# A mixture-of-experts loop on Trainium2: four expert loads ahead of the first gathers, and pair weights computed from visit 50 on

## The chip, the cores and the metric

The kernel runs on one core of a Trainium2 chip. A core has TensorE (matmuls, PE in the profile; its weight loads are PEld), VectorE (DVE), ScalarE (ACT), GpSimd (POOL) and SyncE (SP), and 16 DMA engines that move data between device memory and the on-chip SBUF. The metric is the device time of one execution in microseconds, less is better. Three runs of the kernel before gave 882.2, 882.6 and 886.55 us: the median is 882.6.

## The reference

The reference is a decoder of two layers on x of 8 sequences, 128 tokens and 256 features, in float32. Only its last part matters here, the mixture of experts over 1024 tokens:

```python
logits = jnp.einsum('th,eh->te', x, gate_w)          # 64 experts
probs = jax.nn.softmax(logits, axis=-1)
topk_w, topk_idx = jax.lax.top_k(probs, 8)
combine = (jax.nn.one_hot(topk_idx, 64) * topk_w[..., None]).sum(axis=1)
def step(acc, inp):
    w13_e, w2_e, c = inp
    g = x @ w13_e[:128].T
    u = x @ w13_e[128:].T
    h = jax.nn.silu(g) * u
    o = h @ w2_e.T
    return (acc + c[:, None] * o, None)
```

After it come the residual sum and a layer norm.

## The kernel before

The kernel computes only the 8192 pairs of a token and one of its eight experts. The pairs are sorted by expert into 64 blocks of 128. A *visit* takes one expert and up to 128 sorted pairs; with a block border inside an expert there are at most 127 visits, and with these inputs 104 are enough (the arm called few; the arm called all is the same with 127).

Ahead of the loop the routing stage works out which token stands in each sorted place (tok_i, L1055), which output row each place has (pairs, L1062), and the expert and start column of each visit (visits). For each pair its place is found again in slot1, and own holds the eight places of a token.

The loop, run_visits (L1103), goes over steps from -8 on. A step can do these things, and each is pipelined against the others:

- **fetch(v)** (L1123) loads an expert's three weight matrices, 384 KB, into a ring of nine tiles (wring, L1067), by a DMA from SP. It runs eight visits ahead, so the first nine fetches wait for nothing but the list of visits. A later one waits until the visit nine before it has used its tile.
- **gather(g)** (L1093) fetches the 128 token rows of block g by an indirect DMA from GpSimd. The first four are issued ahead of the loop, into tiles of their own (xg_first); the rest go into a ring of six (xg_few).
- **turn(g)** (L1117) transposes a gathered block on TensorE, and VectorE copies it to cols, the sorted columns.
- **hidden(v)** (L1136) does gate and up on TensorE (8 matmul records), silu on ScalarE, and the product hid (moe_h_few, L1152) on VectorE.
- **down(v)** (L1155), two steps later, does the last matmuls (4 records) and ScalarE copies the result back to cols (L1162).
- **turn_back(g)** (L1166), from step 43 on, transposes a finished block on TensorE, VectorE copies it to moe_os, and an indirect DMA from GpSimd scatters its rows to pair_rows in device memory.
- **weight(b)** and **spread(b)** (L1070, L1085), at every twelfth step, compute for sequence b on VectorE the weights of its pairs: eq (two 128x512 operations, L1072 and L1076), a reduction to pair_weight (L1079), and five 128x128 diagonal matrices, diag (L1087).

TensorE's and GpSimd's orders in the loop are as written (manual_schedule, L1182). VectorE's is not: a scheduler places its instructions by when their inputs are ready. The inputs of weight(b) are ready before the loop, so all eight groups stand among the first twenty or so visits there, with two eq ahead of the first copy to cols. In TensorE's order turn(0) and turn(1) stand ahead of hidden(0); behind it come turn(2), hidden(1), turn(3), hidden(2), turn(4) and down(0).

Behind the loop the tail reads pair_rows back (z), sums the eight rows of each token with the weights, and finishes. It uses diag and pair_weight.

Of the kernel before, what the change touches and what calls it, by code (L numbers as in the profile page):

```python
# [14 lines left out]
ALU = mybir.AluOpType  # L15
# [3 lines left out]
B = 8  # L19
# [15 lines left out]
NG = B * S * TOP // P  # L35
NV = NG + NE - 1
AHEAD = 4
FEW = 104
FAR = 65536.0
MIDDLE = (P - 1) / 2  # L40
# [19 lines left out]
def decoder_kernel(ctx: ExitStack, tc: tile.TileContext, i, out):  # L60
    nc = tc.nc
# [23 lines left out]
    def ps_mm(name):  # L85
        return ps_of["mm"].tile([P, 512], F32, tag="mm", name=name)

    def ps_tr(name):
        return ps_of["tr"].tile([P, 512], F32, tag="tr", name=name)

    def ps_o(name):
        return ps_of["o"].tile([P, 512], F32, tag="o", name=name)
# [389 lines left out]
    with l0, tc.tile_pool(name="l0a", bufs=2) as ap:  # L482
# [4 lines left out]
        qT, kT, v = [], [], []  # L487
# [582 lines left out]
    def weight(b):  # L1070
        eq = wk.tile([P, TOP, NE], F32, tag="e", bufs=6, name=f"eq_{b}")
        nc.vector.tensor_tensor(  # L1072
            eq, slot1[:, b, :].unsqueeze(1).to_broadcast([P, TOP, NE]),
            own[:, b, :].unsqueeze(2).to_broadcast([P, TOP, NE]), ALU.is_equal,
        )
        nc.vector.tensor_tensor(  # L1076
            eq, eq, comb[:, b, :].unsqueeze(1).to_broadcast([P, TOP, NE]), ALU.mult
        )
        nc.vector.reduce_sum(cw[:, b, :], eq, axis=AX.X)  # L1079
# [5 lines left out]
    def spread(b):  # L1085
        for k in range(ON_PE):
            nc.vector.tensor_scalar(diag[:, b, k, :], ident, cw[:, b, k : k + 1], None, ALU.mult)  # L1087

    def turned(step):

        return min(max(step + 3 + max(step, 0) // 4, 0), NG)

    def gather(g, arm, x=None):  # L1093
        if x is None:
            x = mp.tile([P, D], F32, tag="xg", bufs=6, name=f"xg_{arm}_{g}")
        nc.gpsimd.indirect_dma_start(  # L1096
            out=x, out_offset=None, in_=xd,
            in_offset=bass.IndirectOffsetOnAxis(ap=tok_i[:, g : g + 1], axis=0),
            bounds_check=B * S - 1, oob_is_err=False,
        )  # L1100
        return x

    def run_visits(arm, count):  # L1103


        spare = count - NG

        def begins(v, engine, after):

            with tc.issue_after(after[-1]) if after else nullcontext():  # L1110
                return nc.values_load(
                    visits[0:1, 1, v : v + 1], engines=[engine],
                    min_val=max(v - spare, 0) * P, max_val=min(v, NG) * P,
                    skip_runtime_bounds_check_because="each visit before takes 128 pairs at the most",
                )

        def turn(g):  # L1117
            pt = ps_tr(f"moe_xT_{arm}_{g}").rearrange("p (k t) -> p k t", k=4)[:, :2]
            for k in range(2):
                nc.tensor.transpose(pt[:, k, :], xg[g][:, k * P : (k + 1) * P], ident)  # L1120
            nc.vector.tensor_copy(cols[:, :, (g + 1) * P : (g + 2) * P], pt)  # L1121

        def fetch(v):  # L1123
            w = wring.tile([P, 3 * D], F32, tag="w", name=f"w_{arm}_{v}")
            with tc.issue_after(fetched[-1]) if fetched else nullcontext():
                e = nc.values_load(
                    visits[0:1, 0, v : v + 1], engines=[nc.sync.engine], min_val=0, max_val=NE - 1,
                    skip_runtime_bounds_check_because="the least of it and the last expert was taken",
                )
                dma = nc.sync.dma_start(  # L1130
                    out=w, in_=i["experts"][:, bass.ds(e, 1), :].rearrange("p e n -> p (e n)")
                )
            fetched.append(dma.ins)
            ws[v] = w

        def hidden(v):  # L1136
            o = begins(v, nc.tensor.engine, fed)
            ps = ps_mm(f"moe_gu_{arm}_{v}")[:, :D].rearrange("p (a t) -> p a t", a=2)
            for a in range(2):
                for k in range(2):  # L1140
                    at = k * D + a * P
                    mm = nc.tensor.matmul(  # L1142
                        ps[:, a, :], ws[v][:, at : at + P], cols[:, k, bass.ds(o + P, P)],
                        start=(k == 0), stop=(k == 1),
                    )

                    tc.declare_no_dep(mm.ins, group=f"left_{arm}", reason="columns of earlier visits")
            fed.append(mm.ins)
            s = mp.tile([P, P], F32, tag="s", name=f"moe_s_{arm}_{v}")
            nc.scalar.activation(s, ps[:, 0, :], AF.Silu)  # L1150
            hid = mp.tile([P, P], F32, tag="hid", bufs=4, name=f"moe_h_{arm}_{v}")
            nc.vector.tensor_tensor(hid, ps[:, 1, :], s, ALU.mult)  # L1152
            hs[v] = hid

        def down(v):  # L1155
            ps = ps_o(f"moe_o_{arm}_{v}")[:, :D].rearrange("p (c t) -> p c t", c=2)
            for c in range(2):
                at = 2 * D + c * P
                nc.tensor.matmul(ps[:, c, :], ws[v][:, at : at + P], hs[v], start=True, stop=True)  # L1159
            o = begins(v, nc.scalar.engine, left)  # L1160

            cp = nc.scalar.copy(cols[:, :, bass.ds(o, P)], ps)  # L1162
            left.append(cp.ins)
            tc.add_to_no_dep_group(f"left_{arm}", cp.ins)

        def turn_back(g):  # L1166
            pt = ps_tr(f"moe_oT_{arm}_{g}")[:, :D]
            for k in range(2):
                nc.tensor.transpose(pt[:, k * P : (k + 1) * P], cols[:, k, g * P : (g + 1) * P], ident)  # L1169
            o = mp.tile([P, D], F32, tag="o", bufs=4, name=f"moe_os_{arm}_{g}")  # L1170
            nc.vector.tensor_copy(o, pt)  # L1171
            inst = nc.gpsimd.indirect_dma_start(  # L1172
                out=zd, out_offset=bass.IndirectOffsetOnAxis(ap=pairs[:, g : g + 1], axis=0),
                in_=o, in_offset=None, bounds_check=B * TOP * S - 1, oob_is_err=False,
            )

            tc.declare_no_dep(inst.ins, group=f"pairs_{arm}", reason="disjoint rows")
            tc.add_to_no_dep_group(f"pairs_{arm}", inst.ins)

        fed, left, fetched = [], [], []  # L1180
        xg, ws, hs = dict(ahead), {}, {}
        with tc.manual_schedule(engines={nc.tensor.engine, nc.gpsimd.engine}):  # L1182
            for step in range(-8, count + 4):
                if 0 <= step < count:
                    hidden(step)
                for g in range(turned(step - 1), turned(step)):
                    turn(g)
                if 0 <= step - 2 < count:
                    down(step - 2)
                if 0 <= step + 8 < count:  # L1190
                    fetch(step + 8)
                while len(xg) < min(turned(step) + 4, NG):
                    xg[len(xg)] = gather(len(xg), arm)
                if 0 <= step - 3 - spare < NG:
                    turn_back(step - 3 - spare)
                if 0 <= step < 12 * B and step % 12 == 11:
                    weight(step // 12)
                    spread(step // 12)

    ahead = {  # L1200
        g: gather(g, "first", wk.tile([P, D], F32, tag=("r", "xb")[g % 2], name=f"xg_first_{g}"))
        for g in range(AHEAD)
    }
    few = nc.values_load(
        visits[0:1, 2, FEW : FEW + 1], min_val=0, max_val=NE,
        skip_runtime_bounds_check_because="a number of experts",
    )
    with tc.If(few == NE) as enough:
        run_visits("few", FEW)
    with enough.Else():  # L1210
        run_visits("all", NV)
# [11 lines left out]
    for b in range(B):  # L1223
        z = zs[b]
        ps = ps_mm(f"moe_sum_{b}")[:, :D]
# [81 lines left out]
```

## Time and profile before

| what | value |
|---|---|
| median of three runs | 882.6 us |
| profiled execution, its own time | 881.06 us |
| its span, first to last instruction | 879.1 us |
| granted TensorE clock, mean | 0.954 |
| TensorE busy | 803.5 us, 91% |
| VectorE busy | 460.3 us, 52% |
| GpSimd busy | 232.9 us, 26% |
| expert loads | 104 of 384 KB |
| first expert load issued | 620.16 us |
| first matmul of visit 0 | 634.51 us |
| last scatter issued | 840.23 us |

Times in the profile count from the start of the span. A row of the timeline has the start, the length, the engine, the line, the operation, the tile written and those read; in brackets stands how long the engine was idle before it and what ended that. A DMA row on SP or GpSimd is the issue of a transfer, not the transfer itself. In a table by stretch the first figures are busy microseconds of each engine with the number of instructions.

### The profile page before, as it was taken

What the parts mean: (1) busy time and instruction counts of PE and PEld (TensorE: products, weight loads), DVE (VectorE), ACT (ScalarE), POOL (GpSimd) and SP (SyncE); (2) the same over time, 40 slices, a digit from 0 to 9 for tenths busy, and PEclk for the clock granted to TensorE, in tenths of its full rate; (3) what the DMA queues carried; (4) which work ended last, traced back from release to release, by engine and by line L of the source; (5) the groups of instructions that cost most, each with busy time, mean ns of one, the idle gap of its engine ahead of it and who ended that gap; (6) DMA issues with size and microseconds to landing.
All of it is one profiled execution on the core that took longest, in us unless ns stands there. A gap on an engine that the chain in (4) does not pass through costs nothing. (4 is left out here: it accounts for less than half of the span.)

```text
span 879.1 us, 14286 instructions
## 1 busy us (share of the span) xinstructions
PE 803.5 (91%) x4588; PEld 539.6 (61%) x4588; DVE 460.3 (52%) x1280; ACT 288.7 (33%) x990; POOL 232.9 (26%) x321
## 2 busy tenths in 40 slices
PE   8899997999999999999999999996588888999945
PEld 5455653667455558555557655553588877988834
DVE  3699886413544442344444566755795333443335
ACT  2567742221333330233330132332232332333301
POOL 0011113215100000000015121101566655555524
PEclk9999987999999999999999998987599999999979
DMA  5500011820000000000000000000579987998665
GB/s 167 157 1 1 2 48 49 293 90 1 0 1 0 1 1 0 1 0 1 1 18 31 1 14 1 13 13 13 198 227 287 296 279 224 299 309 290 203 237 228
DMA packets 39730, 87.80 MB, mean 100 GB/s; under 512 B 6432, under 2 KB 16192, under 8 KB 38752
## 3 DMA queue, kind: packets, MB, share of 16 engines
q1 hardware_dynamic: 32352, 68.96, 24.0%
q0 software_dynamic: 6144, 16.79, 5.7%
q10 hardware_dynamic: 1152, 1.05, 0.4%
q8 instruction: 41, 0.67, 0.3%
q14 instruction: 41, 0.34, 0.1%
HBM read 76.29 MB, written 10.49 MB: 99 GB/s over the span
## 5 line engine op out<-in xcount | busy, mean ns | idle before, releaser
L224 ACT ACTIVATE l_e<-l_s,nm_l 128x128 f32<-128x128 f32 x256 | 90.4, 370 | 93.2 <-DVE nm_l L221 92.9
L1142 PE MATMUL moe_gu_few<-cols,w_few 128*128 (+1 forms) x832 | 114.0, 281 | 2.2 <-issue 0.4
L1142 PEld LDWEIGHTS moe_gu_few<-cols,w_few 128*128 128x128 f32 x832 | 102.9, 195 | 7.5 <-issue 6.6
L1172 POOL DMA_INDIRECT pair_rows<-moe_os_few,pairs x64 | 63.3, 988 | 53.3 <-DVE moe_os_few L1171 41.1
L1096 POOL DMA_INDIRECT xg_few<-x_rows,tok_i x60 | 62.8, 1047 | 29.5 <-issue 11.3
L1159 PE MATMUL moe_o_few<-moe_h_few,w_few 128*128 128x128 f32 x416 | 63.9, 276 | 0.0
L843 ACT ACTIVATE y_e<-y_sT 128x512 f32<-128x512 f32 x64 | 33.0, 603 | 83.3 <-PE y_sT L836 50.6
L740 PE MATMUL l_q<-xT_l1a,w_qkv 128*128 128x512 f32 x128 | 60.2, 593 | 0.0
L740 PE MATMUL l_k<-xT_l1a,w_qkv 128*128 128x512 f32 x128 | 60.1, 592 | 0.0
L740 PE MATMUL l_v<-xT_l1a,w_qkv 128*128 128x512 f32 x128 | 60.1, 592 | 0.0
L231 DVE TENSOR_SCALAR l_e<-l_e,inv_l 128x128 f32<-128x128 f32 x256 | 58.3, 292 | 1.4
L723 DVE TENSOR_TENSOR l_vs<-l_c,l_vs 128x512 f32<-128x512 f32 x32 | 22.1, 692 | 67.4 <-PE l_c L722 67.4
L1162 ACT COPY cols<-moe_o_few 128x256 f32 (+1 forms) x104 | 38.9, 374 | 55.2 <-PE moe_gu_few L1142 18.7
L703 PE MATMUL l_y<-w_o,l_vs 128*128 128x256 f32 x256 | 56.9, 381 | 0.0
L1150 ACT ACTIVATE moe_s_few<-moe_gu_few 128x128 f32<-128x128 f32 x104 | 28.9, 279 | 79.9 <-PE moe_gu_few L1142 39.8
L1159 PEld LDWEIGHTS moe_o_few<-moe_h_few,w_few 128*128 128x128 f32 x416 | 55.2, 193 | 0.0
L703 PEld LDWEIGHTS l_y<-w_o,l_vs 128*128 128x128 f32 x256 | 48.2, 190 | 9.8 <-issue 2.8
L224 ACT ACTIVATION_READ_ACCUMULATOR l_e<-l_s,nm_l 128x1 f32 x256 | 53.2, 208 | 0.0
L1121 DVE COPY cols<-moe_xT_few 128x256 f32<-128x256 f32 x64 | 26.5, 417 | 48.2 <-PE moe_o_few L1159 21.4
L1152 DVE TENSOR_TENSOR moe_h_few<-moe_gu_few,moe_s_few 128x128 f32<-128x128 f32 x104 | 29.7, 286 | 41.5 <-ACT moe_s_few L1150 25.6
L221 DVE TENSOR_REDUCE nm_l<-l_s 128x4 f32<-128x512 f32 x64 | 43.2, 684 | 10.0 <-PE l_s L755 8.1
L748 ACT COPY l_vs<-l_v 128x512 f32<-128x512 f32 x32 | 18.8, 586 | 78.4 <-PE l_v L740 78.4
(267 smaller groups left out, 1360.0 us busy)
## 6 DMA issues: line engine op xcount, KB each, us to landing
w_few<-in_experts SPq DMA_DIRECT2D x104, 384.0 KB
z<-pair_rows SPq DMA_DIRECT2D x7, 1024.0 KB
w_qkv<-in_w_qkv SPq DMA_DIRECT2D x8, 768.0 KB
w_o<-in_w_o SPq DMA_DIRECT2D x1, 2048.0 KB
xT<-in_xT SPq DMA_DIRECT2D x2, 512.0 KB
x<-in_x SPq DMA_DIRECT2D x4, 256.0 KB
cx<-in_ctx SPq DMA_DIRECT2D x1, 1024.0 KB
q_up<-in_up_qT SPq DMA_DIRECT2D x4, 256.0 KB
```

The lines of the kernel that those rows point to most:

```text
L221: nc.vector.tensor_reduce(nm, s, AX.X, ALU.max, negate=True)
L224: nc.scalar.activation(e[:, a, :], s[:, a, :], AF.Exp, bias=nm[:, a : a + 1], scale=1.0, accum_out=sums[:, a : a + 1],)
L231: nc.vector.tensor_scalar(e[:, a, :], e[:, a, :], inv[:, a : a + 1], None, ALU.mult)
L703: nc.tensor.matmul(py[:, :D], scaled[b // 4, m][:, b % 4 * S : (b % 4 + 1) * S], w_o[:, m, :], start=(m == 0), stop=(m == L1_HEADS - 1),)
L740: nc.tensor.matmul(ps, w_qkv[:, k, c, n, :], xT[h][:, k, :], start=(k == 0), stop=(k == 1))
L843: nc.scalar.activation(e, tiles[j], AF.Exp)
L1096: nc.gpsimd.indirect_dma_start(out=x, out_offset=None, in_=xd, in_offset=bass.IndirectOffsetOnAxis(ap=tok_i[:, g : g + 1], axis=0), bounds ...
L1142: mm = nc.tensor.matmul(ps[:, a, :], ws[v][:, at : at + P], cols[:, k, bass.ds(o + P, P)], start=(k == 0), stop=(k == 1),)
L1152: nc.vector.tensor_tensor(hid, ps[:, 1, :], s, ALU.mult)
L1159: nc.tensor.matmul(ps[:, c, :], ws[v][:, at : at + P], hs[v], start=True, stop=True)
L1162: cp = nc.scalar.copy(cols[:, :, bass.ds(o, P)], ps)
L1172: inst = nc.gpsimd.indirect_dma_start(out=zd, out_offset=bass.IndirectOffsetOnAxis(ap=pairs[:, g : g + 1], axis=0), in_=o, in_offset=None, ...
```

## The change

It has three parts, and the rest of the kernel is as before.

First, fetch(4) is preceded by a memset of one element of its tile on GpSimd. In GpSimd's order this stands behind the four gathers of xg_first and ahead of the first one of xg_few. The load overwrites the element, so it has to wait for the memset; the fetches behind it on SP follow it.

Second, weight and spread of sequence b move from step 12b + 11 to step 50 + 6b, that is to steps 50, 56, up to 92.

Third, each such group is placed behind the product hid of the latest visit in VectorE's order (issue_after of the last entry of gated). Otherwise the scheduler orders VectorE as before.

```diff
+PROMPT = 4
...
         def fetch(v):
             w = wring.tile([P, 3 * D], F32, tag="w", name=f"w_{arm}_{v}")
+            if v == PROMPT:
+
+                nc.gpsimd.memset(w[0:1, 0:1], 0.0)
             with tc.issue_after(fetched[-1]) if fetched else nullcontext():
...
-            nc.vector.tensor_tensor(hid, ps[:, 1, :], s, ALU.mult)
+            gated.append(nc.vector.tensor_tensor(hid, ps[:, 1, :], s, ALU.mult).ins)
...
-        fed, left, fetched = [], [], []
+        fed, left, fetched, gated = [], [], [], []
...
-                if 0 <= step < 12 * B and step % 12 == 11:
-                    weight(step // 12)
-                    spread(step // 12)
+                if 0 <= step - 50 < 6 * B and (step - 50) % 6 == 0:
+
+                    with tc.issue_after(gated[-1]):
+                        weight((step - 50) // 6)
+                        spread((step - 50) // 6)
```

In VectorE's order of the changed kernel the first instruction of the loop is a copy to cols; each group then stands as hid, eq, a copy to moe_os, eq times combine, the reduction, the next hid, and five diag.

## The prediction

> **What bounds the kernel now.** I read the page's chain of waits first, then a table of busy time in stretches, then the timeline of the stretch where the expert loop starts. The chain puts the loop's matmuls first, but it begins with a transfer of experts, a gather, and VectorE:
>
> ```profile
> 622.93 3.65 DMA w_few<-in_experts
> 626.62 0.62 POOL xg_first L1096
> ...
> 628.24 5.75 DMA xg_first<-x_rows,tok_i
> ...
> 634.03 0.70 PE moe_xT_few L1120 x2
> 635.18 1.20 DVE eq L1076 x2
> ...
> 638.38 0.98 DVE diag L1087 x5
> ```
>
> Columns: start, length, what. A gather issued at 628.24 has landed only at 633.99, and from there VectorE's work on the pair weights (eq, diag) is on the chain. The table by stretch (window, length, then busy us of PE, PEld, DVE, ACT, POOL, then the granted clock, DMA share, GB/s):
>
> ```profile
> 620.00:630.00 10.00, 5.36 (x44) 5.03 (x42) 7.70 (x16) 2.90 (x4) 3.17 (x4) 0.50 0.82 282
> 630.00:640.00 10.00, 6.29 (x37) 5.60 (x38) 5.85 (x18) 1.76 (x4) 7.87 (x8) 0.65 0.52 182
> 640.00:650.00 10.00, 9.52 (x81) 8.98 (x81) 9.21 (x30) 3.11 (x10) 6.41 (x7) 1.00 0.71 207
> 650.00:660.00 10.00, 7.73 (x64) 6.88 (x62) 10.00 (x31) 3.06 (x10) 7.27 (x7) 1.00 0.84 277
> 660.00:690.00 30.00, 27.25 (x232) 25.87 (x232) 15.03 (x50) 9.35 (x31) 19.97 (x20) 1.00 0.91 292
> ```
>
> VectorE is full from 640 to 660 and half idle afterwards. The timeline of GpSimd's and VectorE's rows there:
>
> ```profile
> 626.62 1.32 POOL L1096 DMA_INDIRECT xg_first<-x_rows,tok_i  x1 [6.22 <-DMA w_few<-in_experts]
> 628.24 1.00 POOL L1096 DMA_INDIRECT xg_first<-x_rows,tok_i  x1 [0.30 <-issue]
> 629.55 1.52 POOL L1096 DMA_INDIRECT xg_first<-x_rows,tok_i  x1 [0.30 <-issue]
> 631.37 1.00 POOL L1096 DMA_INDIRECT xg_first<-x_rows,tok_i  x1 [0.30 <-issue]
> 632.67 1.00 POOL L1096 DMA_INDIRECT xg_few<-x_rows,tok_i  x1 [0.30 <-issue]
> ...
> 651.09 1.70 POOL L1096 DMA_INDIRECT xg_few<-x_rows,tok_i  x1 [0.83 <-PE moe_gu_few L1142]
> ```
>
> The reader is to see that gathers go out back to back, one per 1.30 us (1.00 and a gap of 0.30), and that some take longer.
>
> Two things that the averages hide. **Expert weights are not what TensorE waits for**: in the trace's packets, from visit 9 on, each expert's 384 KB land 5.7 us or more before its visit. And **VectorE is hardly what sets the pace**: starts of visits in the trace are 2.01 us apart from visit 4 to 18 (669.95 - 641.87, over 14), where VectorE is full, and still 1.94 from 18 to 42 (716.59 - 669.95, over 24), where it isn't. What remains there is the ring of six gather buffers: a gather lands about 3.7 us after its issue, TensorE turns it two or three us later, and GpSimd waits 0.8 to 1.0 us for that every two or three gathers. After visit 50 visits are 1.74 us apart.
>
> **Part 1: loads 4 to 8 behind the first gathers.** Before, the nine loads that fill the ring are issued between 620.16 and 627.41, so gather 0 (issued 626.62) is in the DMA queues with loads 5 to 8 and lands at 631.98, 5.4 us after its issue. Gather 5, issued at 633.98 when the loads were done, took 2.4 us. After, load 4 waits for a memset that stands in GpSimd's queue behind the four gathers. Nothing else stands on SP behind load 4 but loads 5, 6 and so on. Loads 0 to 3 land by 626.18 as before, so gather 0 meets empty queues and lands at about 629.0, gather 1 (628.24) at 630.7, gather 2 at 632.0, gather 3 (issued 630.9, since gather 2 loses its excess of 0.5) at 633.3.
>
> The memset: a 1x1 one is not in the trace; the nearest row is GpSimd's 128x256 memset of cols, 0.31 us, so it costs between 0 and 0.6 us with its gap. With it gather 4 goes out near 632.3, where it went at 632.67. Load 4 starts near 632.2 and lands, with the 3.6 us that load 4 takes now, near 636; its visit is at 641.87 now, at about 639 after. The cover shrinks from 14 us to 3. Load 8 follows at 635.9 and lands by 642 for a visit near 646.
>
> Down the path: transposes 0 and 1 go from 633.16 and 634.03 to about 629.2 and 630.8, visit 0 from 634.36 to about 631.3. Then the table load on ScalarE (1.28 us) and the first two hid follow. Ahead of visit 0's second matmuls in TensorE's order stands the transpose of gather 4, now at 639.32. That gather now travels among loads 4 and 5: 2.4 us if they leave it alone, 5.4 at worst, so it lands between 634.7 and 637.7; I take 636.2, by the middle of both rows. Gain there: 3.0 us (1.5 to 4.0).
>
> Here a rule speaks against the change. The Trainium skill, "DMA: Bandwidth & Descriptors", section "SWDGE vs HWDGE vs iDMA", says that inside each DMA engine the software and the hardware queues are different ones and taken in turn. By it a gather passes the backlog of loads, and part 1 would win little, at most the doubled transfer time, 0.7 us. The row says otherwise: gather 0's first packet starts 3.9 us after its issue, gather 5's 1.7. I go by the row: 3.0 and not 0.7.
>
> **Part 2: pair weights away from visits 0 to 20.** Removed there are 8 groups of eq (0.68), eq times combine (0.67), reduce (0.67) and 5 diag (0.28): spaced as they are (0.60 and 0.20), 2.8 us each, 22 us of VectorE. By the pace of visits this is worth (2.01 - 1.94) x 14 = 0.9 us; the bounds are 0 and 2.3 us, the sum by which gathers 10 to 22 exceed 1.00. I take 0.9. What is late next is the ring of gathers, which doesn't change.
>
> **Part 3: the same groups behind visits 50, 56, ... 92.** The copies of gathers into cols end at 739.5, so VectorE is 15.7 us busy in the 65 us from 741 to 806 (TensorE's copies back and hid), and a group adds 2.8 us to each 10.4. In the changed order eq stands behind hid(50), then one copy to moe_os, eq times combine and reduce, hid(51), 5 diag. hid(51) is late by up to 1.2 us and one copy by 0.7. In the trace a regular visit has 2.0 us between the start of hid and the matmul that needs it (hid of visit 74 at 781.75, its matmul at 784.35), and a scatter has 1.25 us of idle GpSimd behind every second one. So most is hidden; without that cover a group costs up to 1.2, eight 9.6.
>
> What is not hidden is GpSimd. Here I weigh the second rule: "SBUF — State Buffer", section "Who interferes with whom", lets tensor_tensor and tensor_reduce leave descriptor generation alone, and makes fp32 tensor_scalar block it. By that the diag instructions would cost: 5 x 0.2 x 8 = 8 us. The rows say that the gather at 651.09 took 1.70 beside an eq (651.24), while the one at 654.83 took 1.00 beside four diag (654.63 to 655.49), and every gather between 663 and 718 took 1.00. The excess over 1.00 of all gathers from the third on is 3.2 us. I take half of it as on the path, since GpSimd is idle in part: **+1.6** (0 to 3.2; 9.6 if VectorE's delays count too).
>
> **Sum**: -3.0 - 0.9 + 1.6 = -2.3 us. The profiled execution took 881.06 (span 879.1), so it would take 878.8; the median shown is 1.5 above it, 882.6, hence **880.3**.
>
> **Rivals.**
> 1. *Both gains are whole and VectorE's late work free*: -4.0 - 2.3 + 0 = -6.3, 876.3. For it: DMA share is 0.52 and 0.71 in the stretches that would fill, and all slack above. Against it: with a full VectorE the pace was only 3% worse.
> 2. *The start doesn't carry*: what gather 0 wins, gathers 4 to 9 lose among the five late loads (5 x 1.3 us of transfer from 632 to 639), and the ring of gathers sets the pace anyway: 0 to -0.5, 882.4.
> 3. *Slower*: from visit 50 VectorE's groups stand between hid and TensorE. TensorE's waits there come in lumps (visit 77 starts 3.0 us after 76, visit 84 3.1 after 83), with ScalarE, VectorE and GpSimd all released together; behind such a lump the cover of 2 us is gone and the whole delay counts. At 1.2 us a group, 9.6 - 3.9 = +5.7: 888.3. It decides from (3.9 + 4.4) / 8 = 1.04 us a group on.
> That the change is undone by a scheduler is no case: in the changed program the groups do stand behind hid 50, 56 and so on, and load 4 has its wait for GpSimd.
>
> **How the numbers follow.** The forecast 0.42, rival 1 0.24, rival 2 0.17, rival 3 0.17. Half a per cent, 4.4 us, is about what a measurement here can tell. Faster is below 878.2: nearly all of rival 1 and a fifth of the forecast, 0.32. Slower is above 887.0: most of rival 3, 0.16. Within: 0.52. The forecast's own range is 877 to 883 (its unknowns: 1.5 to 4.0, 0 to 2.3, 0 to 3.2). To leave out no more than 2 in 10 the range reaches through rival 1 and most of rival 3: 874.5 to 888.5.
>
> **What would show it.** Right: the first gather landed before 630, transposes 0 and 1 before 631, visit 0 before 632, transpose 4 near 636; load 9 near 638 rather than 641.45; gathers between 641 and 661 all at 1.00; visits 4 to 18 at 1.95 us; scatters of 1.2 to 1.7 beside eq after visit 50, and visits 50 to 92 at most 0.05 us slower each. Wrong: transpose 4 after 638.5 (part 1), visit 42 less than 3 us earlier than now (part 2), or the time from visit 50 to 103 (94.4 us now) longer by more than 4 us (part 3).

## The result, and the profile after

The changed kernel took **886.45 us** (median of 20 runs) beside 882.0 us for the kernel before (20 runs): a ratio of 1.0058, 95% interval 1.0040 to 1.0077. It is slower by 0.6%, where the prediction said 880.3 and no change. The profiled execution took 887.66 us.

The same stretches as before (length, then busy us of PE, PEld, DVE, ACT, POOL, then the granted clock, DMA share, GB/s):

```profile
620.00:630.00 10.00, 5.49 (x43) 4.92 (x40) 6.20 (x13) 2.90 (x4) 3.19 (x4) 0.50 0.55 183
630.00:640.00 10.00, 6.38 (x38) 5.52 (x38) 2.28 (x6) 1.84 (x3) 7.22 (x9) 0.84 0.79 253
640.00:650.00 10.00, 10.00 (x77) 10.00 (x77) 3.75 (x12) 3.26 (x11) 5.67 (x6) 0.83 0.80 243
650.00:660.00 10.00, 9.22 (x79) 8.60 (x78) 3.13 (x11) 2.84 (x10) 6.28 (x7) 1.00 0.91 298
660.00:690.00 30.00, 26.20 (x221) 24.65 (x221) 11.24 (x36) 9.52 (x32) 18.94 (x19) 1.00 0.90 285
```

VectorE (third figure), which was full from 640 to 660, is now busy for a third. Yet TensorE does 77 and 79 matmul records there, where it did 81 and 64, and from 660 to 690 it does 221, where it did 232. From 640 to 690 that is 377 records in both: the room on VectorE turned into nothing.

The start of the loop, from the timeline of all engines:

```profile
630.66 0.69 PE L1121 MATMUL moe_xT_few<-ident,xg_first 128*128 128x128 f32 x2 [0.52 <-DMA xg_first<-x_rows,tok_i]
631.14 1.92 PE L1146 MATMUL moe_gu_few<-cols,w_few 128*128 128x128 f32 x8
631.45 0.09 POOL L1128 MEMSET w_few<- 1x1 f32 x1
...
633.19 1.06 PE L1146 MATMUL moe_gu_few<-cols,w_few 128*128 x8
...
634.55 0.41 PE L1121 MATMUL moe_xT_few<-ident,xg_first 128*128 128x128 f32 x2 [0.30 <-issue]
...
635.29 1.13 PE L1146 MATMUL moe_gu_few<-cols,w_few 128*128 x8 [0.32 <-DVE moe_h_few L1156]
...
637.80 0.28 ACT L1154 ACTIVATE moe_s_few<-moe_gu_few 128x128 f32<-128x128 f32 x1 [3.01 <-PE moe_o_few L1163]
...
639.27 0.42 DVE L1122 COPY cols<-moe_xT_few 128x256 f32<-128x256 f32 x1 [0.87 <-remote]
...
639.75 1.95 PE L1146 MATMUL moe_gu_few<-cols,w_few 128*128 x8 [2.44 <-issue]
640.80 0.28 ACT L1154 ACTIVATE moe_s_few<-moe_gu_few 128x128 f32<-128x128 f32 x1 [2.73 <-PE moe_gu_few L1146]
```

Visit 0 starts 3 us earlier than before, as forecast. Then look at visit 1: its eight records start at 633.19 and end at 634.25 by the profile's model, and ScalarE, idle from 634.79, starts the silu on them only at 637.80, 3.5 us after that end. For visit 2 (635.29 to 636.42) it is 640.80, 4.4 us. VectorE is late in the same way: it copies transpose 3, which ended at 634.96, to cols only at 639.27 (the trace can't name who ended that wait). Visit 3 needs this copy, so it waits until 639.75, and the lead is gone. Its eight records then take 1.95 us in place of 1.06: the granted clock was 0.51 from 640.0 to 643.4, where it was 1.00 before.

The late stretch, as one row each: before first, then after (740 to 833, between visits 50 and 103 in both).

```profile
740.00:833.00 93.00, 87.89 (x732) 82.15 (x731) 36.78 (x105) 32.38 (x104) 51.26 (x52) 1.00 0.85 278
```

```profile
740.00:833.00 93.00, 83.88 (x690) 77.44 (x689) 53.77 (x162) 31.01 (x98) 49.38 (x49) 1.00 0.88 273
```

VectorE has 17 us more to do, and TensorE gets 690 records done in place of 732. The visits behind one late group (it began at 751.41 with eq behind hid, and ended at 755.75 with the last diag), from the timeline:

```profile
758.50 1.06 PE L1146 MATMUL moe_gu_few<-cols,w_few 128*128 x8
...
760.95 0.61 PE L1163 MATMUL moe_o_few<-moe_h_few,w_few 128*128 128x128 f32 x4
762.18 0.28 ACT L1154 ACTIVATE moe_s_few<-moe_gu_few 128x128 f32<-128x128 f32 x1 [3.21 <-PE moe_o_few L1163]
...
762.76 0.37 ACT L1166 COPY cols<-moe_o_few 128x256 f32 x1 [0.31 <-ACT moe_s_few L1154]
...
763.19 0.44 PE L1173 MATMUL moe_oT_few<-ident,cols 128*128 128x128 f32 x2 [1.63 <-ACT cols L1166]
```

Again silu begins 2.6 us after the modelled end of its matmuls (759.56), the copy to cols comes behind it, and TensorE, whose transpose of a finished block needs that copy, stands for 1.63 us. Where all this went is plain when the starts of visits are counted from the first expert load (us):

| | visit 0 | 4 | 18 | 42 | 50 | 103 | visits 50 to 103 |
|---|---|---|---|---|---|---|---|
| before | 14.21 | 21.71 | 49.79 | 96.44 | 119.24 | 213.64 | 94.40 |
| after | 11.15 | 22.79 | 49.46 | 97.07 | 119.33 | 219.52 | 100.19 |

Up to visit 50 nothing is won, and then 5.8 us are lost.

### The profile page after: what moved, and what is told of

It is laid out like the page before. It is cut to its first block, busy times and chain, and to the rows that moved or that the text cites. A ratio compares the mean times of both kernels' runs of the same rounds, so it can differ in the third digit from the quotient of the medians.

```text
span 885.7 us, 14292 instructions
## 1 busy us (share of the span) xinstructions
PE 804.0 (91%) x4588; PEld 539.1 (61%) x4588; DVE 458.3 (52%) x1280; ACT 288.6 (33%) x990; POOL 230.4 (26%) x322
## 5 line engine op out<-in xcount | busy, mean ns | idle before, releaser
L1176 POOL DMA_INDIRECT pair_rows<-moe_os_few,pairs x64 | 64.3, 1005 | 58.3 <-DVE moe_os_few L1175 28.4
L1097 POOL DMA_INDIRECT xg_few<-x_rows,tok_i x60 | 59.9, 999 | 33.5 <-PE moe_gu_few L1146 15.3
L1166 ACT COPY cols<-moe_o_few 128x256 f32 (+1 forms) x104 | 38.8, 373 | 50.6 <-PE moe_o_few L1163 16.6
```

The costliest lines, as they stand in the source:

```text
L1097: nc.gpsimd.indirect_dma_start(out=x, out_offset=None, in_=xd, in_offset=bass.IndirectOffsetOnAxis(ap=tok_i[:, g : g + 1], axis=0), bounds ...
L1176: inst = nc.gpsimd.indirect_dma_start(out=zd, out_offset=bass.IndirectOffsetOnAxis(ap=pairs[:, g : g + 1], axis=0), in_=o, in_offset=None, ...
```

## The experiments

The ratio is always against the kernel before, run beside it on the same chip, with its 95% interval. The experiments ran on five chips. The kernel before took 880.9, 878.4 and 877.7 us on those of the first, second and fourth, but 853.9 and 853.5 on those of the third and fifth. That turned out to be the key, so stages are compared within one kind of chip only. "Late" below means: silu begins more than 0.8 us after the modelled end of its gate and up matmuls.

### First chip: the parts alone

**The start alone** (groups at every twelfth step as before, memset kept).

> The kernel before with the memset alone (loads 4 to 8 behind the first gathers); the pair weights stand where they stood. Bunching theory (GpSimd's indirect DMAs, standing back to back while other DMA traffic runs, hold back TensorE's completions): visit 0 starts about 3 us earlier than before, the lead is lost again by visit 5 to a wait at visits 3 and 4, visits 50 to 103 take 94 to 95 us as before, total -1.5 to +1 us. If the lead had been lost to the late groups alone, the total would be 3 us below before. If the memset is what made the kernel slower, it is 4 to 6 us above before.

Measured: 0.9998 (0.9980 to 1.0015). Visit 0 stands at 11.18 us and visit 4 at 22.44: the lead is lost between them. Visits 50 to 103 took 96.10 us, a little over the 94 to 95 expected. Part 1 is worth nothing.

**The late groups alone** (the changed kernel without its memset).

> The changed kernel without the memset: all nine loads in front again, pair weights from visit 50. Bunching theory: visits 50 to 103 take 99 to 101 us as in the changed kernel (94.4 before), visits 4 to 42 save about 1 us, total 4 to 5.5 us above before. If memset and late groups share the loss, the total is 1 to 3 us above before.

Measured: 1.0055 (1.0030 to 1.0080), visits 50 to 103 100.38 us. The whole loss is here.

**No groups.** The groups are left out, and diag and pair_weight set to zero behind the loop, so the experts' sum is missing from the output.

> The changed kernel with the eight groups of pair weights left out; diag and pair_weight are set to zero behind the loop, in time that VectorE waits for pair_rows, so the experts' sum is left out of the output. Both the bunching theory and the direct theory (VectorE's groups make TensorE wait for hid): visits 50 to 103 back to 93 to 95 us, total 5 to 7 us below the changed kernel, about 0 to 1.5 us below before. If the longer end is due to the shifted start (memset) and not to the groups, visits 50 to 103 stay at 98 to 101 us.

```diff
     loop.close()
+    nc.vector.memset(diag, 0.0)
+    nc.vector.memset(cw, 0.0)
```

Measured: 1.0040 (1.0022 to 1.0059). The scheduler put the 128x5120 memset (4.33 us) at 605.3, ahead of the routing's work on VectorE, so the total says nothing. Visits 50 to 103 took 95.32.

**Groups in lumps, but early** (behind hid at steps 6, 11, to 41).

> The changed kernel with the groups at steps 6, 11, ... 41 instead of 50, 56, ... 92, each still behind the latest hid. Bunching theory: visits 50 to 103 take 94 to 95 us; in visits 6 to 42 the gathers wait for TensorE and not for VectorE, so a group costs at most 0.3 us there: total -1 to +2 us against before. Direct theory: a group costs its 0.7 us there too, the total stays 4 to 6 us above before.

Measured: 1.0051 (1.0035 to 1.0066). Visit 50 is at 123.17 (119.33 in the changed kernel), and visits 50 to 103 take 95.45. Against the start alone, which has the same memset, the early lumps cost 3.5 us (885.68 - 882.21); against the kernel before, the late ones cost 4.5 (885.43 - 880.92). So a lump costs at both places, as the direct theory had it and the bunching theory had not.

### Second chip: what of a late group costs

**No groups, cleanly**: loads as before, the two memsets behind the last copy to moe_os.

> Loads at the start as in before, the groups of pair weights left out altogether (diag and pair_weight are set to zero by two memsets behind the last copy to moe_os, beside the last scatter), so the output is not the reference's. It gives the price of the late groups by difference, with nothing moved ahead of the loop. Theory (the late groups cost about 5 us): visits 50 to 103 take 94 to 96 us, as in before and 4 to 6 less than in the changed kernel; visits 4 to 18 take 1.90 us each; all in all 0.998 of before (880 to 881). Rival (the 5 us come from something else in the late stage, such as where the loads stand in the ring): visits 50 to 103 take 99 us or more here too, and the ratio is 1.003 or more.

Measured: 1.0005 (0.9984 to 1.0026), visits 50 to 103 94.77, visits 4 to 18 1.85 us each (2.005 in before), but visit 4 at 23.38 (21.71). The ratio expected was 0.998. So on this chip, where the groups stood before, they cost nothing that shows in the time, and there was nothing to win by moving them.

**The same, with scatters four at a time**:

> The same without groups, but GpSimd's scatters are put out four at a time: each fourth turned block sends its own scatter and those of the three before it; moe_os has eight buffers. VectorE does nothing more than in the run without groups. Theory H (a row of scatters without pause holds back what TensorE reports to ScalarE and VectorE; the late groups cost what they cost because they bunch the scatters): visits 50 to 103 take 98 us or more, with waits of TensorE of 1 to 2 us at each row of four, and the ratio is 1.003 or more. Theory D (the groups stand in front of hid and of the copies to moe_os on VectorE, and that alone is what TensorE waits for): visits 50 to 103 stay within 1 us of the run without groups, 94 to 96.

```diff
+            held.append((g, o))
+            if len(held) < HELD and g < NG - 1:
+                return
+            for g, o in held:
...
```

Measured: 0.9974 (0.9962 to 0.9987), visits 50 to 103 93.96. Theory H, that the scatters need only stand in rows to do harm, falls: here they helped a little.

**Groups taken apart**, one part behind each hid from visit 50 to 89:

> The groups are taken apart: behind the hid of each visit from 50 to 89 stands one part only (eq; eq times combine; the reduction; three diag; two diag), five visits for a sequence. The same work on VectorE in the same stretch, at most 0.84 us between two hid in place of 1.2 to 2.8. Loads as in before. If the cost is that of lumps (delay beyond TensorE's cover, or bunched scatters): visits 50 to 103 take 94.5 to 97 us and the ratio is 1.000 or less. If it is the sum of VectorE's time, or GpSimd's longer scatters beside eq: 98.5 us or more and 1.003 or more.

```diff
-                if 0 <= step - 50 < 6 * B and (step - 50) % 6 == 0:
+                if 50 <= step < 50 + 5 * B:
                     with tc.issue_after(gated[-1]):
-                        weight((step - 50) // 6)
-                        spread((step - 50) // 6)
+                        part((step - 50) // 5, (step - 50) % 5)
```

Measured: 0.9996 (0.9979 to 1.0014), visits 50 to 103 94.99. The same work in the same stretch costs nothing when it isn't in a lump. That excludes the sum of VectorE's time, and the longer scatters beside eq, as the cost.

**Loads from the fourth on behind gather 7** (groups as before):

> Groups at every twelfth step as in before; the memset that lets load 4 go stands behind gather 7 in place of gather 3, so gathers 4 to 7 go out with no load of an expert in flight. If the stall at visits 3 and 4 (4.5 and 2.8 us in the changed kernel) comes from gathers going out back to back while loads are in flight: visit 3 starts at most 2.5 us after visit 2, transpose 4 goes within 2.5 us of its gather's landing time of about 635, and visit 4 stands at 20 to 21.5 us from the first load (22.4 with the memset behind gather 3, 21.7 in before), unless load 4 itself is late, which shows as a wait for w_few. If the stall is that of the gathers alone or of ScalarE's table load: visits 3 and 4 stay where they were, 22.4 or later. Ratio by the first 0.998, by the second 1.000 to 1.002.

Measured: 1.0006 (0.9991 to 1.0021). The memset is at 635.96 and load 4 goes out at 636.13. Silu of visit 1 is on time and visit 3 starts 1.6 us after visit 2, as the first theory has it; but silu of visit 2, due at 635.14, begins at 638.28, and visit 4 starts 4.8 us after visit 3, at 21.86. The stall moved back by one visit and did not go. It was already there for a microsecond when the load went out, so whether loads have a part in it is left open; in the time nothing is won.

### Third chip: the same lumps where ends are not late

**The kernel before with scatters in fours**, **whole late lumps with scatters in fours** (loads as before), **the weights in a lump with one diag a visit**, and **the weights one a visit with the diag in a lump**:

> The kernel before, with its groups at every twelfth step and its loads as they are, and only GpSimd's scatters put out four at a time with eight buffers for moe_os. The run without groups gained 0.3% by that. If the gain belongs to the scatters alone: ratio 0.9975 (0.996 to 0.999), visits 42 to 50 take 20.5 us (22.8 in before) and 50 to 103 at most 94. If it needed VectorE's free time at the start: 1.000.

> The late groups in lumps as in the changed kernel, loads as in before, and scatters four at a time with eight buffers for moe_os. Theory G (a lump costs because the copies to moe_os are held back, the scatters then stand in a row and hold each other and what waits for GpSimd): with scatters in rows anyway and eight buffers the lumps cost at most 1 us, visits 50 to 103 take 94 to 95.5, ratio 0.9975. Theory D (hid or the copies come too late for TensorE, whatever GpSimd does): visits 50 to 103 take 98.5 us or more, ratio 1.003.

```diff
                 if 0 <= step - 50 < 6 * B and (step - 50) % 6 == 0:
                     with tc.issue_after(gated[-1]):
                         weight((step - 50) // 6)
                         spread((step - 50) // 6)
...
+            held.append((g, o))
+            if len(held) < HELD and g < NG - 1:
+                return
```

> Loads as in before. In place of a whole group behind hid 50, 56 and so on, the eq, eq times combine and the reduction stay together (2.04 us between two hid, with one copy to moe_os among them), and the five diag follow one a visit. If the three operations of the weights are what costs (hid late by 1.2 us): visits 50 to 103 take 98.5 to 100 us and the ratio is 1.004 or more. If it needs the whole lump, or the diag: 94.5 to 96.5, ratio 1.000.

```diff
+                if 50 <= step < 50 + 6 * B:
+                    b, n = divmod(step - 50, 6)
+                    with tc.issue_after(gated[-1]):
+                        if n == 0:
+                            weight(b)
+                        else:
+                            spread(b, n - 1)
```

> The counterpart: eq, eq times combine and the reduction stand one a visit, and the five diag together (1.06 us, one copy to moe_os among them). If the diag cost (GpSimd held by fp32 tensor_scalar, or the copy behind them): visits 50 to 103 take 98 us or more. If the weights do: 94.5 to 96 and ratio 1.000.

```diff
+                if 50 <= step < 50 + 6 * B:
+                    b, n = divmod(step - 50, 6)
+                    with tc.issue_after(gated[-1]):
+                        part(b, n)
```

Measured: 0.9974 (0.9961 to 0.9987), **0.9931** (0.9907 to 0.9955), 0.9942 (0.9917 to 0.9967) and 0.9950 (0.9930 to 0.9970). The last three are lower than any theory had said. Visits 50 to 103 take 83.16, 83.11, 83.80 and 83.70 us, against 94 to 100 so far, and the lump costs nothing. The timeline of the whole late lump with fours, at its first group:

```profile
720.75 0.68 DVE L1074 TENSOR_TENSOR eq<-slot,own 128x512 f32<-128x512 f32 x1
721.35 0.42 DVE L1173 COPY moe_os_few<-moe_oT_few 128x256 f32<-128x256 f32 x1
...
722.25 1.06 PE L1144 MATMUL moe_gu_few<-cols,w_few 128*128 x8
...
723.00 0.28 DVE L1154 TENSOR_TENSOR moe_h_few<-moe_gu_few,moe_s_few 128x128 f32<-128x128 f32 x1
...
723.35 0.28 ACT L1152 ACTIVATE moe_s_few<-moe_gu_few 128x128 f32<-128x128 f32 x1 [0.61 <-PE moe_gu_few L1144]
...
723.81 1.06 PE L1144 MATMUL moe_gu_few<-cols,w_few 128*128 x8
...
724.71 0.50 PE L1161 MATMUL moe_o_few<-moe_h_few,w_few 128*128 128x128 f32 x3
```

Silu begins at 723.35, 0.04 us after the modelled end of its matmuls (723.31). Hid is late by the group, at 723.00 with silu done at 722.07, but the matmul that needs it is due only at 724.71: the cover that the prediction counted on is there. TensorE starts a visit every 1.56 us and does not wait. The same in one row for 81 us:

```profile
720.00:801.00 81.00, 81.00 (x725) 80.66 (x725) 56.20 (x168) 33.85 (x104) 52.68 (x52) 1.00 0.92 320
```

725 records in 81 us without a pause, at the same granted clock of 1.00 as the 690 in 93 us of the changed kernel. In the four profiles of this chip silu is late at visit 0 alone (the table load); from visit 50 on its mean delay is 0.04 us. In the profile of the kernel before at the head of this document it is late at 23 of the 24 visits from 18 to 41 and at 7 of the 54 from 50 on; in the changed kernel at 24 and 15.

The other finding is on the start: with the groups at the start (scatters in fours) visits 4 to 18 take 1.91 us each and visit 50 stands at 103.30; with late groups 1.71 and 99.30. On this chip the groups' early place did cost 4 us.

### Fourth chip: the lumps where ends come late

> The changed kernel once more, beside the next three. Theory L (a lump costs only where TensorE's ends are reported late): where silu begins 0.1 us or less after its matmuls, visits 50 to 103 take 83 to 84.5 us, as in the last runs, and the ratio is 0.992 to 0.996; where it begins 1 us or more after them at ten or more of the visits from 50 on, they take 99 to 100.5 and the ratio is 1.005. Rival (the lump of a whole group always costs, the last runs were free because their lumps were smaller or their scatters came in fours): 4 us more than the run with the spread groups of this batch, whatever silu does.

> Whole lumps, scatters four at a time with eight buffers, on the chip of this batch. Theory L: as the changed kernel, so 98.5 us or more for visits 50 to 103 where silu begins late, 83 to 84.5 where it doesn't. Theory G (scatters held one behind the other by late copies to moe_os make the cost): at least 3 us less than the changed kernel for visits 50 to 103 where silu begins late there.

> The weights in a lump, diag one a visit, on the chip of this batch. Where silu begins late, the size of the lump decides: 97 to 100 us for visits 50 to 103 and 1.003 or more if 2 us of VectorE are enough, 94.5 to 96 and 1.000 if only the whole lump costs. Where silu doesn't begin late: 83 to 84.5 and 0.994, as in the run before.

**Spread groups and scatters in fours**:

> One part of a group behind each hid from visit 50 to 89, and scatters four at a time: both edits that cost nothing or gained alone. If their effects add: 0.9975 where silu begins late (the gain of the scatters), 0.993 or less where it doesn't (that of VectorE's free time at the start too).

| kernel | median, us | ratio (95%) | visits 50 to 103 | late from visit 50 on |
|---|---|---|---|---|
| changed kernel | 883.49 | 1.0063 (1.0043 to 1.0084) | 99.43 | 18 |
| whole lumps, fours | 881.62 | 1.0032 (1.0013 to 1.0052) | 100.63 | 18 |
| weights in a lump | 878.41 | 1.0011 (0.9994 to 1.0027) | 95.73 | 8 |
| spread, fours | 876.59 | 0.9990 (0.9975 to 1.0005) | 94.46 | 4 |

Theory L holds, and theory G falls: the very kernel whose lumps were free on the third chip loses 6.2 us here against the one with spread groups (100.63 - 94.46), 5.0 by the medians, 0.63 us a group. Both have their scatters in fours and no memset. (The changed kernel's own time on this chip would not have told theory L from its rival.) Most of the loss shows at one group of instructions, the transposes of finished blocks. Columns: busy us, mean ns, then TensorE's idle time ahead of them and who ended it; whole lumps with fours on this chip (736 to 834), then the spread groups with fours (736 to 827), then the whole lumps on the third chip (720 to 801):

```profile
L1171 PE MATMUL moe_oT_few<-ident,cols 128*128 128x128 f32 x104 | 20.7, 280 | 8.2 <-ACT cols L1164 7.8 <-issue 0.4
```

```profile
L1172 PE MATMUL moe_oT_few<-ident,cols 128*128 128x128 f32 x102 | 20.3, 281 | 1.6 <-ACT cols L1165 1.0 <-issue 0.5
```

```profile
L1171 PE MATMUL moe_oT_few<-ident,cols 128*128 128x128 f32 x104 | 19.9, 273 | 0.0
```

7.8, 1.0 and 0.0 us of waiting for ScalarE's copies to cols: 6.8 us between the first two kernels, about what the visits lost. (Where TensorE waits is not always the same place: the spread groups with single scatters, on the second chip, also waited 6.6 us there, and less ahead of the gate and up matmuls. The time of the visits is the firm figure.) A lump of the weights alone (2.04 us of VectorE, single scatters) stands 1.3 us above the spread groups by the visits, and by the time nothing that can be told: the cost of 5 us needs the whole group. The effects of the spread groups and of the fours did not surely add: 0.9975 was expected, 0.9990 measured.

### Fifth chip: what makes the ends late

> The kernel before, with each finished block written by a plain DMA from SP to consecutive rows in place of GpSimd's scatter (the rows stay unsorted, so the output is not the reference's). No indirect DMA is left from visit 56 or so on; the bytes are the same. If GpSimd's indirect DMAs make TensorE's ends late, and the chip is one where they are: silu begins 0.1 us after its matmuls from visit 56 on and visits 50 to 103 take 83 to 86 us (94.4 in before). If they don't: as before, 93 to 96, with silu 1 us or more late at five visits or more. On a chip without late ends: 83 to 84 in any case.

```diff
-            inst = nc.gpsimd.indirect_dma_start(
-                out=zd, out_offset=bass.IndirectOffsetOnAxis(ap=pairs[:, g : g + 1], axis=0),
...
+            inst = nc.sync.dma_start(out=zd[g * P : (g + 1) * P, :], in_=o)
```

> The kernel before, but from visit 50 on no expert is loaded: the visits use the nine tiles of visits 41 to 49 in turn (the output is not the reference's). GpSimd's scatters stay. If loads in flight make TensorE's ends late, or make the scatters' descriptors slow, and the chip is one where they are late: silu begins 0.1 us after its matmuls from visit 52 on and visits 50 to 103 take 83 to 86 us. If the scatters alone do it: 93 to 96. If both are needed, this run and the one with SP's writes both fall to 83 to 86. If neither matters, both stay at 93 to 96, and what is left is TensorE itself.

```diff
         def fetch(v):
+            if v >= 50:
+                ws[v] = ws[41 + (v - 41) % 9]
+                return
```

Measured: 0.9977 (0.9963 to 0.9992) and 0.9986 (0.9972 to 1.0001). This chip was of the second kind: silu was never late but at visit 0, visits 50 to 103 took 82.63 and 82.59. So neither run could tell what makes ends late; what the traces show of it stands in the last section. The two do show that on such a chip neither GpSimd's scatters nor the expert loads hold the late stage: with both, on the third chip, it took 83.2 us, and TensorE hardly paused.

## Why the prediction was wrong

**Part 1's first steps were right, its gain was not.** The first gather landed at 628.99 (forecast 629.0), transposes 0 and 1 went at 629.45 and 630.66, visit 0 at 630.93, and transpose 4 at 636.42 (forecast 636); only load 9, at 640.90, was 3 us later than said. With no loads ahead of it gather 0's first packet came 2.0 us after its issue (3.9 before), so the reading of the row held, and not what was made of the rule weighed there. The step that failed is "Gain there: 3.0 us (1.5 to 4.0)": what a gain at visit 0 is worth at the end was taken for the gain itself. By visit 3 it was gone, because ScalarE and VectorE took up TensorE's results 3.5 to 4.4 us late. The start alone measured 0.9998. Rival 2 had the outcome, not the mechanism: gathers 5 and 6 had landed at 637.13 and 638.12, and were turned at 641.28 and 643.83, so it was not they that TensorE waited for.

The clock is a term that the sum does not have. Five of the six profiles with the memset show a stretch of 3.4 or 6.8 us at a granted clock of 0.5 that begins 8.8 to 12.3 us after visit 0; none of the fourteen without it does. It is not what loses the lead: the sixth, the first of the runs without groups, shows no such stretch and has visit 4 at 23.19.

**Part 2's 0.9 us came and went.** The gathers from 641 to 661 all took 1.00, and visits 4 to 18 took 1.905 each, as expected or better. But visit 42 came 0.6 us later in place of 3 earlier (from the first load), and without any groups the time is 1.0005. The step that failed is the reading that the ring of gather buffers sets the 1.94 us of visits 18 to 42: on the third chip the same ring allows 1.61 to 1.67. What stood in that stretch was silu, 1 to 2.5 us late at nearly every visit. It takes VectorE's place as soon as VectorE is free: in visits 9 to 17 silu was late once before, and eight times after. Where it isn't late, the prediction erred the other way: VectorE did set the pace, and 4 us were to be had, not 0.9 or 2.3.

**Part 3 was mis-sized: +1.6 was forecast, about +5 was measured** (5.8 between the two profiles, 5.0 by the medians on the fourth chip). The step that failed is "What is not hidden is GpSimd". A scatter took 1005 ns in the mean after and 988 before, about 1 us over all 64, and the spread groups have the same scatters (1007 ns) at no cost. Hid itself stayed covered, as the prediction said. TensorE's groups from 740 to 833, two of before and then the same two of after, with its idle time ahead of them last:

```profile
L1159 PE MATMUL moe_o_few<-moe_h_few,w_few 128*128 128x128 f32 x208 | 31.7, 275 | 0.0
L1169 PE MATMUL moe_oT_few<-ident,cols 128*128 128x128 f32 x104 | 20.7, 280 | 3.7 <-ACT cols L1162 3.2 <-issue 0.5
```

```profile
L1163 PE MATMUL moe_o_few<-moe_h_few,w_few 128*128 128x128 f32 x197 | 30.1, 275 | 0.0
L1173 PE MATMUL moe_oT_few<-ident,cols 128*128 128x128 f32 x98 | 19.3, 279 | 7.2 <-ACT cols L1166 6.2 <-issue 1.1
```

Ahead of the matmuls that read hid (moe_o) TensorE never waited. What grew is its wait for ScalarE's copies to cols ahead of the transposes, a path through late silu that the prediction put at nothing. Counted from the starts of all records between visits 50 and 103 (0.112 us apart where nothing is waited for), the waits ahead of the transposes grew from 5.1 to 9.6 us, those at gate and up from 5.6 to 7.0, which together is about the loss.

Two readings in that part are off, too. The 15.7 us of VectorE from 741 to 806 are the copies to moe_os alone; with hid they are 26.4. The two times given for visit 74 are 2.6 us apart, not 2.0. The rule of the Trainium skill, "SBUF — State Buffer", section "Who interferes with whom", by which fp32 tensor_scalar such as diag can block descriptors, is not borne out either: in the spread kernel 14 scatters stand beside diag alone and took 0.98 each, while those beside eq alone took up to 1.40.

Rival 3 had the outcome and the kind of place, waits in lumps in which ScalarE, VectorE and GpSimd are all released together. Its mechanism, "the cover of 2 us is gone and the whole delay counts", is not what the trace shows: the first hid behind a lump has 1.7 us from its start to its matmul, in the changed kernel (visit 51) as on the third chip, where the lumps cost nothing. That its 888.3 lies close is in part luck: 1.2 us a group was too much (0.63 measured), and the gains of 3.9 set against it did not exist.

That a lump and late ends together make the loss is shown, by one kernel on two kinds of chip and by the spread groups. How a lump brings about more late ends (15 from visit 50 on, 7 before) is not: the spread groups with single scatters also had 15, and lost nothing. How much of a late end is passed on to TensorE must differ, and no run here took that apart.

**A version that beats both?** Scatters four at a time gained 0.26% twice, once without groups and once on a chip without late ends. With spread groups, on a chip with late ends, they came to 0.999 (0.9975 to 1.0005), 0.8% under the changed kernel (876.59 and 883.49) but not surely under the kernel before. On a chip without late ends whole late groups with fours gained 0.7%. The changed kernel itself was not run on such a chip.

## What to carry to other kernels

Work that is moved into an engine's idle time is better put there in small parts: here the same eight groups cost 5 us in lumps of 2.8 us and nothing one part a visit (at most 0.84 us). That the direct consumer of a delayed result has cover does not mean that the other paths have: hid was never waited for, the copy to cols was. Look first at how long after its matmuls the engine that reads TensorE's result begins, because a loop in which that is late gives back what is gained at its head. And a change worth half a per cent may change its sign with the chip (the whole late lumps with fours: 1.0032 and 0.9931), so compare stages on one chip only.

## What was not expected of the hardware

On three chips, and on that of the first profiles too by its trace, ScalarE and VectorE take up TensorE's results 1 to 6 us after the modelled end of the matmuls, at most visits from 18 to 42 and at some later. On two others they do it within 0.04 us, and the kernel before takes 853.5 to 853.9 us in place of 877.7 to 882.0. The granted clock is the same (mean 0.954 in the first profile of before and in that of before with fours on the third chip), the first expert load goes out at nearly the same time (620.16 and 617.97), and the tail behind the last scatter takes 38.8 and 38.4 us: nearly the whole difference lies in the expert loop.

The ends of matmuls are modelled, but the trace has the times at which TensorE's reports arrive, the updates of the semaphore that the other engines wait for. Behind the late group shown above none arrives from 759.91 to 762.15, then five within 0.25 us, for matmuls that had begun between 759.28 and 761.29. So TensorE worked on, and it is the reports that are late. In the expert loop two reports stand less than 0.09 us apart 126 times in the kernel before and 146 times in the changed one; in the profiles of the third and fifth chips it never happens. The matmuls that they report began at least 0.2 us apart.

They are late while GpSimd's indirect DMAs run. In those that follow another one with no wait between, the kernel before has 2.4 modelled ends of reporting matmuls per us but only 0.9 reports; before with fours on the third chip has 2.4 of both. (One report in seven of the former isn't in the trace, which is far too few to make this difference.) That is a tie in time, not yet a cause: the run that takes the indirect DMAs away came to a chip without late ends. Why the chips differ is open.
